# Layer 1 of a four-layer network: Silu of u and of the gate as x(1 + tanh(x/2))/2, the last product on VectorE, the halves in weights

## The chip, the core and the metric

The kernel runs on one core of one Trainium2 chip. The metric is the device time of one execution in microseconds, from start to end. Five engines work beside each other, each with its own queue in its own fixed order: PE (TensorE, matrix products), DVE (VectorE), ACT (ScalarE, which evaluates functions from tables), POOL (GpSimd) and SP (SyncE, which issues transfers). Matrix results lie in PSUM, everything else that engines work on lies in SBUF.

## The reference, cut to what matters

Four layers follow each other on an image tensor of 4 x 64 x 64 pixels with 192 channels, each as x + layer(groupnorm(x)). Layers 0 and 3 scan the image in four directions over its whole length, layer 2 multiplies with Toeplitz matrices. Layer 1, in which the change lies, runs one small state-space block over every row and every column, forwards and backwards, so in four directions:

```python
def mamba_block(xs, in_w, cw, cb, xw, dtw, dtb, Alog, Dv, ow):
    xz = jnp.einsum('nlc,dc->nld', xs, in_w)
    u, z = jnp.split(xz, 2, axis=-1)                 # 384 channels each
    ...                                              # 4 taps along the line
    uc = silu(uc + cb[None, :, None])
    x_dbl = jnp.einsum('nld,ed->nle', uc, xw)
    dt, Bp, Cp = jnp.split(x_dbl, [DT_RANK, DT_RANK + DS], axis=-1)
    delta = jax.nn.softplus(jnp.einsum('nlr,dr->nld', dt, dtw) + dtb)
    A = -jnp.exp(Alog)
    # per step: h = exp(delta * A) * h + (delta * u) * B ;  y = sum over 16 states of h * C
    y = jnp.moveaxis(ys, 0, 1) + uc * Dv
    y = y * silu(z)
    return jnp.einsum('nld,cd->nlc', y, ow)
```

silu(x) is x * sigmoid(x), which is x(1 + tanh(x/2))/2. The four results are concatenated and multiplied with one more weight, fc_w; the kernel multiplies fc_w into each out_w beforehand. All data are 32-bit floats.

## The kernel before, in words

Layer 1 is the method mamba. It first normalises x and stores it by rows and by columns, and builds the four combined output weights both_w (lines 737 to 747). Then it works through 128 chunks: four directions, four images, eight chunks of 512 pixels (eight lines of 64). A chunk is a job (mamba_job). Its 384 channels lie in three tiles t of 128.

A chunk has 24 units (t, p, c), one for each half tile of 64 channels and each of four groups of states. A unit is one scan over 128 x 1024 elements, and passes through the engines like this:
- feed (line 354): for 18 of the 24 units PE multiplies the matrices diag with dtuT into the PSUM tile b (line 378; two such buffers exist), and ACT computes dA = exp(delta * A) twice, 504 elements each (line 401), into one of three fixed SBUF tiles. For the other six ("direct") units POOL has multiplied delta * u with B into the SBUF tile bs (line 351), and ACT writes dA into the PSUM tile b.
- scan (line 411): DVE runs the recurrence into h, one of seven buffers; then POOL multiplies h with C in place (line 422).
- collect (line 447): PE sums over the states into y.

Around the units lie the steps of a chunk, each at a number of units counted from the chunk's first (the table when and the list steps, lines 896 to 901). Negative numbers lie in the time of the chunks before, so that several chunks are under way at once. The steps that matter here:
- input_of (steps -36, -34, -31): PE projects a tile of u into in_ps, and ACT scales it by the last tap (line 822). One step later DVE adds the three other taps from PSUM (line 827). Another step later ACT applies Silu with the bias conv_b (line 833).
- project (-24, line 209): PE multiplies u with x_w, which gives dt, B and C.
- finish (-14): ACT applies Softplus to delta (line 271), and POOL forms dtu = delta * u (line 278). In layers 0 and 3 the same line runs on DVE.
- gate (-6, -4, -1): PE projects a tile of the gate into z_ps. One step later ACT applies Silu (line 843).
- gated, after the last scan of a tile: DVE forms u * D + y (line 856, y in PSUM), POOL multiplies with z (line 857).
- out (33, 35): PE multiplies with the combined output weight into o_ps (line 881), and the result goes to memory through an SBUF tile of the name o.
- weights (-50 of a direction's first chunk) loads the direction's weights, and neg_exp turns A into -exp(A) (lines 453 and 454, ACT and DVE).

in_ps, z_ps, o_ps, the projections of step sizes and the transposes share two PSUM buffers (the pool mm). The pool pin has two buffers for each name, so two for o.

The order in which the work is written out follows the steps; a scheduler then fixes each engine's queue when the program is built. Where ACT needs a function whose table isn't loaded, an ACT_TABLE_LOAD stands in front of it in ACT's queue, under the line of the function.

Of the kernel before, what the change touches and what calls it, by code (L numbers as in the profile page):

```python
# [7 lines left out]
F32 = mybir.dt.float32  # L8
AF = mybir.ActivationFunctionType
ALU = mybir.AluOpType  # L10
# [9 lines left out]
T = 512  # L20
# [16 lines left out]
class Kernel:  # L37
# [670 lines left out]
    def mamba(self, x_in):  # L708

        tc, nc, ins = self.tc, self.nc, self.i  # L710
        P, NT = 128, 3
        DI = P * NT
        pre = "L1_"
        by_row, by_col = self.image_tiles("m_row"), self.image_tiles("m_col")
        done = [[self.dram.tile([C, L], F32, name=f"m_out{i}_{b}") for b in range(B)] for i in range(2)]

        both_w = [self.dram.tile([P, NT, C], F32, name=f"m_both_w{i}") for i in range(4)]
        bufs = dict(c=5, bc=2, diag=4, both=4, dtu2=3)
        with (
            tc.tile_pool(name="n", bufs=2) as pn,  # L720
            tc.tile_pool(name="n_ps", bufs=2, space=PSUM) as psum,
        ):
            for b in range(B):
                x = pn.tile([PC, KC, L], F32, name="x")
                for k in range(KC):
                    nc.sync.dma_start(x[:, k, :], x_in[b][:, k, :])
                self.group_norm(x, pn, psum)
                nc.sync.dma_start(by_row[b], x)
                xt = pn.tile([PC, KC, L], F32, name="xt")
                for k in range(KC):  # L730
                    nc.vector.tensor_copy(
                        xt[:, k, :].rearrange("p (a b) -> p a b", b=HW),
                        x[:, k, :].rearrange("p (a b) -> p b a", b=HW),
                    )
                nc.sync.dma_start(by_col[b], xt)
            fw = self.load(pn, "fw", ins["L1_fc_w"], bufs=1)
            for i, part in enumerate((4, 6, 0, 2)):
                ow = self.load(pn, "ow", ins["L1_out_w"][i])
                both = pn.tile([P, NT, C], F32, name="both_w")
                for t in range(NT):  # L740
                    ps = psum.tile([P, C], F32, name="both_ps")
                    for k in range(KC):
                        nc.tensor.matmul(
                            ps, ow[:, k, t * P : (t + 1) * P], fw[:, part + k, :], start=k == 0, stop=k == KC - 1
                        )
                    nc.scalar.copy(both[:, t, :], ps)
                nc.sync.dma_start(both_w[i], both)

        with (
            tc.tile_pool(name="m_once", bufs=1) as once,  # L750
            tc.tile_pool(name="m_w", bufs=2) as pw,
            tc.tile_pool(name="m_in", bufs=2) as pin,
            tc.tile_pool(name="m_prep", bufs=2) as prep,
            tc.tile_pool(name="m_work", bufs=2) as work,
            tc.tile_pool(name="m_c", bufs=bufs["c"]) as cp,
            tc.tile_pool(name="m_bc", bufs=bufs["bc"]) as bcp,
            tc.tile_pool(name="m_diag", bufs=bufs["diag"]) as dp,
            tc.tile_pool(name="m_both", bufs=bufs["both"]) as both,
            tc.tile_pool(name="m_dtu2", bufs=bufs["dtu2"]) as dtu2,
            tc.tile_pool(name="m_mm", bufs=2, space=PSUM) as mm,  # L760
            tc.tile_pool(name="m_b", bufs=2, space=PSUM) as bp,
            tc.tile_pool(name="m_y", bufs=2, space=PSUM) as yp,
        ):
            pools = {"prep": prep, "work": work, "c": cp, "diag": dp, "both": both, "mm": mm, "b": bp, "y": yp,
                     "bc": bcp, "dtu2": dtu2, "bufs": bufs, "behind": 3, "lag": 1}
            fixed = [once.tile([P, 2 * T], F32, name=f"dA{j}") for j in range(3)]
            zero = once.tile([P, 2 * ROWS], F32, name="zero")
            nc.gpsimd.memset(zero, 0.0)
            jobs = []
            for i in range(4):  # L770
                rev, w = i % 2 == 1, {}
                xs = by_row if i < 2 else by_col
                for b in range(B):
                    for c in range(NCH):
                        begin = b == 0 and c == 0
                        jobs.append(self.mamba_job(
                            pw, pin, mm, i, begin, rev, w, xs[b], done[i // 2][b], both_w[i], c, fixed, zero
                        ))
            self.run_jobs(jobs, pools)
        return list(zip(*done))  # L780

    def mamba_job(self, pw, pin, mm, i, begin, rev, w, x, done, both_w, c, fixed, zero):

        nc, ins = self.nc, self.i
        P, NT = 128, 3
# [3 lines left out]
        job = {}  # L789

        def weights():
            for name in ("in_w", "conv_w", "conv_b", "A", "D", "x_w", "dt_b"):
                w[name] = self.load(pw, name, ins[pre + name][i])
            w["dtw"] = self.load(pw, "dt_w", ins[pre + "dt_w"][i])
            w["out_w"] = self.load(pw, "out_w", both_w)
            w["xw"], w["dtb"] = w["x_w"], w["dt_b"]
            self.neg_exp(w["A"])

        def load():
            job["xn"] = self.load(pin, "xn", x[:, :, s])  # L800
            job["u"] = pin.tile([P, NT, T], F32, name="u", bufs=3)

        def project(t, to, name):
            ps = mm.tile([P, T], F32, name=f"{name}_ps", tag="mm")
            for k in range(KC):
                for half in range(2):
                    first = to + t * P + half * 64
                    nc.tensor.matmul(
                        ps[half * 64 : (half + 1) * 64, :], w["in_w"][:, k, first : first + 64], job["xn"][:, k, :],
                        start=k == 0, stop=k == KC - 1,  # L810
                    )
            return ps
# [3 lines left out]
        def input_of(t):  # L816
            ps = project(t, 0, "in").rearrange("p (a b) -> p a b", b=HW)
            u = job["u"][:, t, :].rearrange("p (a b) -> p a b", b=HW)
            tap = lambda j: w["conv_w"][:, t, j : j + 1]

            def taps():
                nc.scalar.activation(u, ps, AF.Identity, scale=tap(3))  # L822
                for j in range(1, 4):
                    to, of = slice(j, HW), slice(0, HW - j)
                    if rev:
                        to, of = of, to
                    nc.vector.scalar_tensor_tensor(  # L827
                        u[:, :, to], ps[:, :, of], tap(3 - j), u[:, :, to], ALU.mult, ALU.add
                    )
                return last  # L830

            def last():
                nc.scalar.activation(u, u, AF.Silu, bias=w["conv_b"][:, t : t + 1])

            return taps

        def gate(t):
            ps = project(t, DI, "z")

            def after():  # L840
                if t == 0:
                    job["z"] = pin.tile([P, NT, T], F32, name="z")
                nc.scalar.activation(job["z"][:, t, :], ps, AF.Silu)

            return after

# [49 lines left out]
        when = dict(project=-24, turn_b=-22, step_size=(-21, -19, -18), finish=-14, turn=(-9, -3, 8), store=-11)  # L896
        each = lambda f, ats: [(at, lambda t=t: f(t)) for t, at in enumerate(ats)]
        steps = [(-50, weights)] if begin else []
        steps += [(-46, load)] + each(input_of, (-36, -34, -31)) + each(gate, (-6, -4, -1)) + each(out, (33, 35))
        if rev:  # L900
            steps += each(earlier, (25, 28))
        job.update(
            P=P, NT=NT, DI=DI, w=w, rev=rev, carry=None, first=True, dA=fixed, y={}, fed={}, done={}, bs={},
# [326 lines left out]
```

## Time and profile before

| | |
|---|---|
| time, median of 3 runs | 30885.05 us (30880.78 to 30885.68) |
| the profiled execution, its own time | 30865.86 us |
| its span, first to last instruction | 30864.0 us |
| mean granted TensorE clock | 0.961 |
| layer 1's chunks, about | 10809 to 21708 us |
| busy in the span: PE, DVE, ACT, POOL | 87%, 72%, 75%, 74% |
| busy in layer 1's chunks (10899 us): PE, DVE, ACT, POOL | 9707, 7956, 9107, 9849 us |

Durations are those of the profiled execution. A line of the groups gives the source line, the engine, the operation, what it writes and reads with shapes, and the count; after the first bar the busy time and the mean duration of one in ns; after the second the time that the engine stood idle just before such instructions, and what ended it. A line of the timeline gives the start in us, the duration in us (of a run of like instructions together), engine, line, operation, tiles, count, and in brackets the idle time before it with its releaser. A line of a stretch gives its bounds and length, then the busy time of PE, PEld (the weight loads of PE), DVE, ACT and POOL with their instruction counts, the granted PE clock, the busy share of the DMA engines and GB/s.

### The profile page before, as it was taken

The numbers are of one execution on the slowest core, as the hardware profiler recorded it, in microseconds if no ns is written. First come the engines' busy times: TensorE is split into PE (matmuls) and PEld (weight loads), VectorE is DVE, ScalarE is ACT, GpSimd is POOL, SyncE is SP. The second block draws the span as 40 slices with busy tenths as digits, with TensorE's granted clock in tenths as the row PEclk, the third lists the DMA queues.
The fourth block names the chain that finished last, engine by engine and source line by source line (L and its number), as shares of the span: only waits on it lengthen the run. The fifth ranks groups of instructions, "written<-read, shape, count | busy, mean of one in ns | idle before, by whom it ended". The sixth has DMA issues, their size and how long they took to land. (4 is left out here: it accounts for less than half of the span.)

```text
span 30864.0 us, 503255 instructions
## 1 busy us (share of the span) xinstructions
PE 26878.4 (87%) x189464; PEld 15827.7 (51%) x189464; DVE 22327.6 (72%) x16587; ACT 23000.6 (75%) x50177; POOL 22890.6 (74%) x9831
## 2 busy tenths in 40 slices
PE   8998998999899688888888888888588988888888
PEld 5664665666466444444444444444355444444444
DVE  7887888788788777777777777777423267777777
ACT  7885886788588588888888888888232278788888
POOL 7885885888588499989998999999100077777777
PEclk9999999999999899999999999999788999999999
DMA  3334333433433533333333333333533345545454
GB/s 109 100 99 117 101 98 104 112 100 99 119 101 97 142 99 97 97 100 101 101 104 97 98 97 99 102 101 102 131 78 76 104 131 131 132 130 134 128 135 128
DMA packets 1652695, 3342.38 MB, mean 108 GB/s; under 512 B 396725, under 2 KB 453494, under 8 KB 1634646
## 3 DMA queue, kind: packets, MB, share of 16 engines
q1 hardware_dynamic: 1541718, 3142.34, 38.1%
q10 hardware_dynamic: 108544, 167.85, 1.6%
q8 instruction: 1497, 24.53, 0.4%
q14 instruction: 936, 7.67, 0.1%
HBM read 2149.81 MB, written 656.08 MB: 91 GB/s over the span
## 5 line engine op out<-in xcount | busy, mean ns | idle before, releaser
L378 PE MATMUL b<-diag,dtuT 128*64 128x256 f32 x98304 | 12607.9, 386 | 1732.9 <-DVE h L411 917.9
L422 POOL TENSOR_TENSOR hc<-h,c 128x1024 f32<-128x1024 f32 x4608 | 10943.4, 2395 | 1515.0 <-DVE h L418 1158.3
L378 PEld LDWEIGHTS b<-diag,dtuT 128*64 128x64 f32 x98304 | 8214.9, 138 | 6212.3 <-DVE h L411 1903.3
L401 ACT ACTIVATE dA<-both,A 128x512 f32<-128x512 f32 (+1 forms) x12288 | 8267.7, 711 | 2124.3 <-DVE h L411 1472.0
L418 DVE TENSOR_TENSOR_SCAN h<-dA,carry,b 128x512 f32<-128x512 f32 x6720 | 8169.8, 1263 | 1367.8 <-PE b L378 861.4
L422 POOL TENSOR_TENSOR h<-h,c 128x1024 f32<-128x1024 f32 x3072 | 7219.1, 2374 | 1049.2 <-DVE h L411 880.3
L332 ACT ACTIVATE diag<-ident,bt 128x128 f32<-128x128 f32 x20480 | 6570.6, 391 | 92.2 <-issue 91.4
L447 PE MATMUL y<-hc,fold 128*64 128x512 f32 x18432 | 5783.3, 599 | 386.1 <-POOL hc L422 384.4
L411 DVE TENSOR_TENSOR_SCAN h<-dA,b 128x1024 f32<-128x1024 f32 x2304 | 5202.8, 2274 | 1147.3 <-ACT dA L401 798.4
L351 POOL TENSOR_TENSOR bs<-dtu,bc 128x1024 f32<-128x1024 f32 x1536 | 3639.4, 2369 | 158.5 <-DMA c<-bc_dram 72.8
L447 PE MATMUL y<-h,fold 128*64 128x512 f32 x12288 | 3259.6, 593 | 10.2 <-POOL h L422 10.2
L501 POOL MEMSET pad<- 128x13068 f32 (+1 forms) x8 | 73.4, 9172 | 3968.3 <-DMA inw<-in_L_in_w 2997.7
L411 DVE TENSOR_TENSOR_SCAN h<-b,bs 128x1024 f32<-128x1024 f32 x768 | 1758.9, 2290 | 1413.6 <-ACT b L401 1102.8
L447 PEld LDWEIGHTS y<-hc,fold 128*64 128x64 f32 x18432 | 1924.0, 138 | 1550.1 <-POOL hc L422 813.1
L401 ACT ACTIVATE b<-both,A 128x504 f32<-128x504 f32 (+1 forms) x3072 | 2076.2, 676 | 376.4 <-DVE h L418 328.3
L418 DVE TENSOR_TENSOR_SCAN h<-b,carry,bs 128x512 f32<-128x512 f32 x1344 | 1639.2, 1260 | 220.9 <-issue 170.4
L237 PEld LDWEIGHTS dtu_ps<-ident,dtu 128*64 128x64 f32 (+1 forms) x16384 | 1183.2, 141 | 497.6 <-issue 375.9
L447 PEld LDWEIGHTS y<-h,fold 128*64 128x64 f32 x12288 | 1005.0, 137 | 795.2 <-issue 444.9
L418 DVE TENSOR_TENSOR_SCAN h<-dA,b 128x512 f32<-128x512 f32 x960 | 1112.8, 1205 | 352.8 <-PE b L378 191.3
L401 ACT ACT_TABLE_LOAD x1019 | 1307.4, 1283 | 11.8
L237 PE MATMUL dtu_ps<-ident,dtu 128*64 128x128 f32 (+1 forms) x16384 | 1272.7, 273 | 45.9 <-DVE dtu L278 41.5
L827 DVE SCALAR_TENSOR_TENSOR u<-in_ps,conv_w,u 128x504 f32<-128x504 f32 (+2 forms) x1152 | 831.6, 722 | 411.7 <-ACT u L822 402.6
(157 smaller groups left out, 24601.4 us busy)
## 6 DMA issues: line engine op xcount, KB each, us to landing
c<-bc_dram SPq DMA_DIRECT2D x3072, 256.0 KB, 4.1
both<-delta SPq DMA_DIRECT2D x2048, 128.0 KB, 2.7
bc<-bc_dram SPq DMA_DIRECT2D x768, 256.0 KB, 4.2
both<-delta_dram SPq DMA_DIRECT2D x1536, 128.0 KB, 3.7
dtu<-dtu_dram SPq DMA_DIRECT2D x1536, 128.0 KB, 2.7
dtu<-dtu SPq DMA_DIRECT2D x1280, 128.0 KB, 2.5
L_y<-out ACTq DMA_DIRECT2D x512, 256.0 KB, 3.0
u<-L_u SPq DMA_DIRECT2D x160, 768.0 KB, 5.4
```

The costliest lines, as they stand in the source:

```text
L237: nc.tensor.matmul(to[half * 64 : (half + 1) * 64], of[:, half * 64 : (half + 1) * 64], self.ident[:p, :p], start=True, stop=True,)
L332: nc.scalar.activation(to, self.ident, AF.Copy, scale=of)
L351: self.nc.gpsimd.tensor_mul(by(b), dtu, by(job["bbc"][p]))
L378: nc.tensor.matmul(to, dtu, job["diag"][p][:, k, 2 * q : 2 * q + 2, :], start=True, stop=True,)
L401: nc.scalar.activation(to[n], of, AF.Exp, scale=w["A"][:, g, 2 * p + n : 2 * p + n + 1])
L411: nc.vector.tensor_tensor_scan(h[:, way], dA[:, way], b[:, way], 0.0, ALU.mult, ALU.add)
L418: nc.vector.tensor_tensor_scan(hn[:, n, way], dA[:, n, way], by_n[:, n, way], start, ALU.mult, ALU.add)
L422: nc.gpsimd.tensor_mul(hc, h, job["cbc"][p])
L447: nc.tensor.matmul(y[c * 64 : (c + 1) * 64, :], self.fold, of, start=first == 0 and n == 0, stop=last == LAST and n == 1)
L501: nc.gpsimd.memset(pad, 0.0)
L827: nc.vector.scalar_tensor_tensor(u[:, :, to], ps[:, :, of], tap(3 - j), u[:, :, to], ALU.mult, ALU.add)
```

## The change

Silu is no longer taken from ACT's table. For u, ACT adds the bias in the first Identity (line 822 before), later computes tanh(u/2) into an SBUF tile of the ring o, and one step later DVE forms (tanh + 1) * u, both from SBUF. For the gate, ACT computes tanh(z/2) from z_ps into z, and one step later DVE forms (tanh + 1) * z_ps, the second input from PSUM. Both results are twice the Silu. The half of u is put into x_w, which DVE halves once for each direction; the remaining uses of u and the gate carry factors of two that the output weight takes back: the 12 evacuations of both_ps multiply by 0.25. (delta * u, like B and C, enters the sum together with x_w's results, so that y is twice what it was, as is u * D.)

```diff
@@ mamba: both_w
-                    nc.scalar.copy(both[:, t, :], ps)
+                    nc.scalar.mul(both[:, t, :], ps, 0.25)
@@ mamba_job: weights
             w["xw"], w["dtb"] = w["x_w"], w["dt_b"]
             self.neg_exp(w["A"])
+            nc.vector.tensor_scalar_mul(w["xw"], w["xw"], 0.5)
@@ mamba_job: input_of
             def taps():
-                nc.scalar.activation(u, ps, AF.Identity, scale=tap(3))
+                nc.scalar.activation(u, ps, AF.Identity, bias=w["conv_b"][:, t : t + 1], scale=tap(3))
...
             def last():
-                nc.scalar.activation(u, u, AF.Silu, bias=w["conv_b"][:, t : t + 1])
+                u = job["u"][:, t, :]
+                half = pin.tile([P, T], F32, name="o")
+                nc.scalar.activation(half, u, AF.Tanh, scale=0.5)
+
+                def doubled():
+                    nc.vector.scalar_tensor_tensor(u, half, 1.0, u, ALU.add, ALU.mult)
+
+                return doubled
@@ mamba_job: gate
-                nc.scalar.activation(job["z"][:, t, :], ps, AF.Silu)
+                z = job["z"][:, t, :]
+                nc.scalar.activation(z, ps, AF.Tanh, scale=0.5)
+
+                def doubled():
+                    nc.vector.scalar_tensor_tensor(z, z, 1.0, ps, ALU.add, ALU.mult)
+
+                return doubled
```

A function that a step returns is called one step later, ahead of that step's own work.

## The prediction

> **What bounds the kernel now.** I read the page first (which engines are busy), then the groups of instructions over the stage that the change touches, then busy time by stretch, then the timeline of one chunk. The stage of layer 1 runs from about 10809 to 21708 us: 128 chunks. GpSimd's product of delta and u comes once a chunk, first at 10789.7 and last at 21597.3 us, so a chunk takes 10807.6 / 127 = 85.1 us. Groups of the stage (line, engine, operation, count | busy, mean ns | idle before, releaser):
>
> ```profile
> L422 POOL TENSOR_TENSOR h<-h,c 128x1024 f32<-128x1024 f32 x3069 | 7212.1, 2374 | 1049.2 <-DVE h L411 880.3 <-PE in_ps L808 155.1 <-PE y L447 12.6
> L401 ACT ACT_TABLE_LOAD x761 | 976.4, 1283 | 8.7
> L843 ACT ACT_TABLE_LOAD x382 | 490.1, 1283 | 6.8
> L833 ACT ACT_TABLE_LOAD x252 | 323.3, 1283 | 4.0 <-DVE u L827 1.1
> L271 ACT ACT_TABLE_LOAD x127 | 162.9, 1283 | 2.3
> ```
>
> Twelve table loads a chunk: six back to Exp, three for the gate's Silu, two for u's, one for Softplus. Next, busy time in one chunk, then in the two stretches of it (stretch, length, PE, PEld, DVE, ACT, POOL):
>
> ```profile
> 14999.38:15084.72 85.34, 76.08 (x550) 39.31 (x552) 62.61 (x39) 71.08 (x133) 77.05 (x34) 1.00 0.35 102
> 15001.70:15051.80 50.10, 44.56 (x330) 24.07 (x328) 37.70 (x24) 37.50 (x70) 50.10 (x23) 1.00 0.36 111
> 15051.80:15084.70 32.90, 29.18 (x200) 13.52 (x197) 22.57 (x15) 32.48 (x63) 24.64 (x12) 1.00 0.35 93
> ```
>
> In the first stretch POOL is never idle. In the second ACT is never idle (32.5 of 32.9 us) and POOL loses 8.3 us. The timeline shows the chain there: ACT is late, the scan waits for it, POOL waits for the scan.
>
> ```profile
> 15066.46 1.28 ACT L843 ACT_TABLE_LOAD   x1
> 15067.76 0.60 ACT L843 ACTIVATE z<-z_ps 128x512 f32<-128x512 f32 x1
> 15070.69 1.28 ACT L401 ACT_TABLE_LOAD   x1
> 15073.33 2.29 DVE L411 TENSOR_TENSOR_SCAN h<-dA,b 128x1024 f32<-128x1024 f32 x1 [4.57 <-ACT dA L401]
> 15082.30 2.29 DVE L411 TENSOR_TENSOR_SCAN h<-b,bs 128x1024 f32<-128x1024 f32 x1 [3.82 <-ACT b L401]
> 15075.70 2.36 POOL L422 TENSOR_TENSOR h<-h,c 128x1024 f32<-128x1024 f32 x1 [2.59 <-DVE h L411]
> 15084.72 2.37 POOL L422 TENSOR_TENSOR h<-h,c 128x1024 f32<-128x1024 f32 x1 [3.80 <-DVE h L411]
> ```
>
> **What the Trainium skill says.** "ScalarE: Activation LUTs", Table sets: Exp and Tanh lie in one set, and a switch of set costs a load of 1283 ns plus a drain of some 1380 ns. The trace agrees on 1283 and shows no such drain: one load, Silu, load takes 3.33 us (15043.90 to 15047.23), 1.30 per load. I use 1.30. "SBUF — State Buffer", Who interferes with whom: a VectorE instruction with two SBUF inputs, or in a two-port mode, excludes a GpSimd instruction that reads SBUF. The trace agrees, with a difference between the two kinds that decides one rival:
>
> ```profile
> 26774.37 2.34 POOL L422 TENSOR_TENSOR hc<-h,c 128x1024 f32<-128x1024 f32 x1
> 26774.79 3.00 DVE L278 TENSOR_TENSOR dtu<-delta,u 96x1024 f32<-96x1024 f32 x1 [0.50 <-ACT delta L271]
> 26776.68 3.34 POOL L422 TENSOR_TENSOR hc<-h,c 128x1024 f32<-128x1024 f32 x1
> 13575.84 8.25 DVE L454 TENSOR_SCALAR A<-A 128x48 f32<-128x48 f32 x1
> ```
>
> The two-input product (1.19 us when undisturbed, the shortest of its line) waited out one POOL instruction, then ran ahead of the next one, which was stretched from 2.37 to 3.34. The tensor_scalar, 0.19 us alone, was passed by four POOL instructions and got in when POOL ran dry.
>
> **The change, part by part.**
> 1. *Loads.* In the instruction order of the changed kernel L401 keeps 383 loads of 1019, L271 its 384, and the two Silu lines' 637 shrink to one. So 10 of 12 loads a chunk go: 10 x 1.30 = 13.0 us of ACT, eight of them (10.4 us) in the second stretch. ACT there falls to about 22 us and stops being what ends last.
> 2. *The functions.* Tanh of the gate is taken at Silu's 597 ns. Tanh of u loses its bias pointer and Identity gains one. No trace row has either form; the difference of Silu with bias from SBUF (722) and without from PSUM (597) bounds it at about 0.12 us each, of opposite sign: 0 net, 0.4 us a chunk at most, covered by ACT's slack.
> 3. *Gate's product on VectorE*, three a chunk. One input is in PSUM, as in L856 (723 ns, some 0.64 start to start): 1.9 us. In one of the two shared PSUM buffers, z_ps is now held until VectorE is done, behind a scan (2.28 us) on its queue; what waits is the next projection on PE, and behind it the b matmuls. Today PE waits 1.2 us a chunk for the gate's Silu. Bounds: -1.2 (the loads ahead of it are gone) to +5.6 (two waits of a scan and a product). I take +0.5.
> 4. *u's product on VectorE*, three a chunk, two SBUF inputs. 0.7 own (L856 has its size), and by L278's example 0 to 2.4 of waiting for the running POOL instruction, 1.1 in the mean: 5.4 us of VectorE a chunk. POOL is held about 0.5 each time, 1.5 a chunk. Below: 0, if POOL is idle at that moment. VectorE comes to 62.6 + 1.9 + 5.4 = 70 us a chunk.
> 5. *x_w halved*, a tensor_scalar from SBUF to SBUF, once per direction; two of four fall into the running stage, as L454's two do. L454 stalled VectorE 8.25 and 7.96 us, after which POOL idled 2.3 + 3.3 us. I take 5.6 each, 11 us in all (0 to 20).
> 6. *Nothing:* the 0.25 goes into the 12 copies of both_ps; the tanh's buffer is the o ring (2 buffers), whose other uses lie at other steps of the chunk, covered by steps of over 3 us between them; the PSUM output of the taps is read no later than before. If the o ring were taken, the wait would be that of a 2 to 3 us store, once or twice a chunk.
>
> No DMA is added or moved past another in the steady part.
>
> **The sum.** POOL's own work sets a floor: 77.05 + 1.5 = 78.5 us a chunk. The second stretch alone can't fall to POOL's 24.6 us, since PE has 29.2 us of work in it and VectorE 22.6 + 1.9 + 3.6 = 28. With only two b buffers these two wait for each other: 29.2 + 0.5 + some 1.3 of mutual waits = 31. If nothing carries over between stretches, a chunk is 2.3 (the instruction ahead of the first stretch) + 50.1 + 0.5 + 31 = 83.9. But POOL enters the second stretch 4.4 us behind VectorE (its queue ends at 15051.84, the scan before at 15047.4), and this lead can grow once ACT isn't late. So a chunk lies between 78.5 and 83.9; I take the middle, 81.2. Gain: (85.1 - 81.2) x 128 = 499 us, less 11 for part 5, is 488. The profiled execution took 30865.9 us (span 30864.0); that gives 30378. The median of the runs, 30885, is 19 above it: 30397.
>
> **Rivals.**
> - *POOL's floor is reached* (22 in 100). For: 50 us without idle in the first stretch, although Softplus's two loads lie in it. Against: PE's 29.2 us. 78.5 us a chunk: 845 - 11 = 834 gained, 30051.
> - *The second stretch stays slow, with VectorE and PE in the place of ACT* (20 in 100). For: 28 and 29.2 us on in-order queues that feed each other. Against: POOL's lead. 83.9 us: 154 - 11 gained, 30742.
> - *Starvation, slower* (8 in 100). u's product is served like L454: only when POOL has run dry. Each then costs POOL 0.64 + 2.28 + 0.1 = 3.0 us (product, next scan, semaphore), three a chunk: 77.05 + 9.1 = 86.1, so +130 us and part 5, 31026; if PE's excess in the second stretch isn't covered by the same idle, up to 90 us a chunk, 31500. It decides from 2.7 us of POOL idle each, (85.1 - 77.05) / 3. For: L454. Against: L278 above, served after one instruction, and L545 beside POOL's copies likewise.
> - *The change doesn't do what it says*, if Tanh lay in another set than Exp: the order above, with its loads gone, excludes it.
>
> **How the numbers follow.** The likeliest case, 80 to 82.4 us a chunk, has 45 in 100 and its own range 30240 to 30550; the floor has 22, the slow stretch 20, starvation 8, and 5 lie about no change (gains of layer 1 lost to a new wait that I don't see). The range 30020 to 30760 leaves out starvation, no change, and the ends of the floor and slow cases. About 0.2%, 62 us, is what a measurement tells from no change; the cases faster by more are 0.45 + 0.22 + 0.20 = 0.87, same 0.05, slower 0.08.
>
> **What would show it.** Right: some 1270 loads fewer; ACT near 58 us a chunk; POOL over 93% busy in the stage; u's product at 0.7 to 3.1 us, with POOL instructions stretched after it; the scan's waits on ACT in the second stretch gone, its waits on PE's b grown. Wrong: products of u of 5 us and more (starvation); PE idle behind the gate's product (part 3 mis-sized); POOL still 90% busy with VectorE busy beside it (the slow stretch).

## The result, and the profile after

The changed kernel takes 30864.08 us in the median (30852.44 to 30871.02, 12 runs), the kernel before beside it 30880.62 (30867.93 to 30888.63, 12 runs). The ratio is 0.9994, with an interval of 0.9986 to 1.0002: no change that a measurement can tell, where a gain of 488 us was forecast. The profiled execution has a span of 30858.5 us, and POOL's product of delta and u comes at 10790.6 the first time and at 21591.1 us the last, so a chunk takes 10800.5 / 127 = 85.04 us, after 85.10.

Yet the loads that the change was to remove are gone. First the groups of the stage, 10809 to 21708 us, as for the kernel before (busy us, mean ns | idle before, releaser):

```profile
L422 POOL TENSOR_TENSOR h<-h,c 128x1024 f32<-128x1024 f32 x3072 | 7325.7, 2402 | 948.3 <-DVE h L411 915.8 <-issue 29.3 <-DMA dtu<-dtu_dram 2.3
L839 DVE SCALAR_TENSOR_TENSOR u<-o,u 128x512 f32<-128x512 f32 x378 | 807.4, 2136 | 0.0
L855 DVE SCALAR_TENSOR_TENSOR z<-z,z_ps 128x512 f32<-128x512 f32 x382 | 257.8, 675 | 238.7 <-ACT z L852 238.7
L271 ACT ACT_TABLE_LOAD x127 | 162.9, 1283 | 2.3
L401 ACT ACT_TABLE_LOAD x127 | 162.9, 1283 | 2.3
```

Two table loads a chunk are left of twelve. L422 still stands idle 916 us for VectorE's scans, where it was 880. And the two new products differ by a factor of three though they do the same arithmetic on the same sizes: 675 ns with one input in PSUM (L855), 2136 ns with both in SBUF (L839).

Busy time in one chunk (length, PE, PEld, DVE, ACT, POOL, PE's clock); the same view before is the chunk from 14999.38 in the prediction:

```profile
15021.16:15106.42 85.26, 76.28 (x550) 38.74 (x548) 70.28 (x45) 58.27 (x123) 77.88 (x36) 0.96 0.35 101
```

ACT has fallen from 71.1 to 58.3 us and VectorE has risen from 62.6 to 70.3, both as the sum said. POOL has 77.9 of 85.3 us, after 77.1. The waits in 12000 to 20000 us (engine and line, what it waited for, total us, times, longest) say what took ACT's place. Three of them before, then those after:

```profile
DVE h L411 <- ACT b L401: 821.8, 302, 4.7
POOL h L422 <- DVE h L411: 654.8, 285, 4.1
DVE h L411 <- ACT dA L401: 574.5, 272, 4.6
```

```profile
PE b L378 <- DVE h L411: 839.5, 340, 6.9
POOL h L422 <- DVE h L411: 667.6, 374, 4.2
DVE h L411 <- ACT b L401: 431.3, 187, 4.4
DVE h L411 <- PE b L378: 299.6, 422, 2.3
DVE h L411 <- ACT dA L401: 54.0, 44, 1.6
```

The scan's waits for ACT were 574.5 (dA) and 821.8 us (b) before, so two thirds of them went. POOL's wait for the scan was 654.8 and is 667.6 us: nothing of what VectorE no longer waits for has reached POOL. The timeline of one chunk shows where it stays (start, duration, engine, line; in brackets the idle time before and its releaser):

```profile
15039.75 7.00 POOL L422 TENSOR_TENSOR h<-h,c 128x1024 f32<-128x1024 f32 x3
15040.41 2.28 DVE L411 TENSOR_TENSOR_SCAN h<-dA,b 128x1024 f32<-128x1024 f32 x1
15042.60 4.71 DVE L839 SCALAR_TENSOR_TENSOR u<-o,u 128x512 f32<-128x512 f32 x1
15047.23 1.50 DVE L828 SCALAR_TENSOR_TENSOR u<-in_ps,conv_w,u 128x504 f32<-128x504 f32 x2
15048.65 2.28 DVE L411 TENSOR_TENSOR_SCAN h<-dA,b 128x1024 f32<-128x1024 f32 x1
15051.00 2.37 POOL L422 TENSOR_TENSOR h<-h,c 128x1024 f32<-128x1024 f32 x1 [4.25 <-DVE h L411]
15050.98 3.68 PE L378 MATMUL b<-diag,dtuT 128*64 128x256 f32 x16 [6.51 <-DVE h L411]
```

POOL has three products in a row, the last ending at 15046.76. VectorE comes to the product of u's first tile at 15042.60, while the second of them runs. It isn't served at 15044.46 when that one ends; the third goes ahead of it, and it ends at 15047.31, when POOL has run dry. Two taps and a scan stand behind it. So POOL idles 4.25 us and PE 6.51 us, until the scan of 15048.65 has read the PSUM tile b. This happens once in each chunk: of the 384 products of u 124 are passed by one POOL instruction in this way and take 4.7 to 5.1 us, one is passed by two (6.9 us), and all but two of the other two tiles' take 0.67 to 0.9.

### The profile page after: what moved, and what is told of

It is laid out like the page before. It is cut to its first block, busy times and chain, and to the rows that moved or that the text cites. A ratio compares the mean times of both kernels' runs of the same rounds, so it can differ in the third digit from the quotient of the medians.

```text
span 30858.5 us, 502565 instructions
## 1 busy us (share of the span) xinstructions
PE 26908.0 (87%) x189464; PEld 15624.6 (51%) x189464; DVE 23308.9 (76%) x17359; ACT 21412.5 (69%) x48905; POOL 23003.0 (75%) x9831
## 4 chain that ended last, share of the span: by engine, by line
PE 35%; DVE 23%; ACT 21%; POOL 8%; issue 6%; DMA 5%; SPq 1%; ACTq 0%; DVEq 0%; POOLq 0%
PE b L378 16%; DVE h L411 9%; ACT dA L401 7%; ACT diag L332 7%; PE y L447 6%; DVE h L418 6%; POOL h L422 4%; DVE u L828 2%; DVE u L839 2%; POOL bs L351 2%; ACT b L401 2%; PE yt_ps L1094 2%; PE conv_ps L533 2%; DMA xn<-t_xn 2%; PE o_ps L1064 1%
## 5 line engine op out<-in xcount | busy, mean ns | idle before, releaser
L422 POOL TENSOR_TENSOR hc<-h,c 128x1024 f32<-128x1024 f32 x4608 | 10947.2, 2396 | 1504.1 <-DVE h L418 1175.8
L422 POOL TENSOR_TENSOR h<-h,c 128x1024 f32<-128x1024 f32 x3072 | 7325.7, 2402 | 948.3 <-DVE h L411 915.8
L447 PEld LDWEIGHTS y<-h,fold 128*64 128x64 f32 x12288 | 898.7, 141 | 670.4 <-issue 332.6
L278 DVE TENSOR_TENSOR dtu<-delta,u 128x1536 f32<-128x1536 f32 (+1 forms) x256 | 563.6, 2202 | 604.9 <-ACT delta L271 604.7
```

The lines of the kernel that those rows point to most:

```text
L422: nc.gpsimd.tensor_mul(hc, h, job["cbc"][p])
L447: nc.tensor.matmul(y[c * 64 : (c + 1) * 64, :], self.fold, of, start=first == 0 and n == 0, stop=last == LAST and n == 1)
```

## The experiments

Had the loads been worth little, or had they been worth what was forecast and something else eaten it? Theory P says the second, and puts the loss into that product of u with two SBUF inputs. Its rivals put it into the added work of VectorE and ScalarE, or into the queue order, which the scheduler fixes anew when instructions change. The recorded expectations call the rivals of a run D and C and say there what each means; Q, R, S and N are named where they come up. "Us a chunk" is the distance of the first and last L278 on POOL, divided by 127; every ratio is against the kernel before on the same chip.

| kernel | median us | ratio, interval | us a chunk |
|---|---|---|---|
| before | 30855 to 30868 | 1 | 85.10 |
| loads_gone | 30256.1 | 0.9804 (0.9789 to 0.9818) | 80.33 |
| psum_half | 30449.6 | 0.9871 (0.9856 to 0.9886) | 81.86 |
| before_plus_add | 31523.7 | 1.0220 (1.0203 to 1.0237) | 90.33 |
| u_only | 30721.6 | 0.9959 (0.9944 to 0.9973) | 84.02 |
| gate_only | 30124.2 | 0.9765 (0.9751 to 0.9780) | 79.25 |
| u_psum_only | 30448.6 | 0.9866 (0.9849 to 0.9882) | 81.81 |
| psum_ring4 | 30446.0 | 0.9864 (0.9849 to 0.9878) | 81.81 |
| gate_ring4 | 30014.3 | 0.9725 (0.9710 to 0.9739) | 78.43 |
| psum_split | 30451.2 | 0.9866 (0.9849 to 0.9882) | 81.87 |
| psum_early | 30463.6 | 0.9870 (0.9855 to 0.9884) | 81.87 |
| gate_split | 30141.3 | 0.9764 (0.9750 to 0.9779) | 79.54 |
| psum_dve_tap | 30035.9 | 0.9732 (0.9715 to 0.9748) | 78.52 |

### The product with one input in PSUM: psum_half

The changed kernel, with tanh(u/2) written into the PSUM buffer in_ps, which is free by then, and not into an SBUF tile. (ACT can do that: in the direct units it writes dA into PSUM too.) The order of VectorE's queue is that of the changed kernel in all but 7 of 17359 places, POOL's in all but 2 of 9831, ACT's in all but 64 of 48905; PE's was not compared. In the cut below flat is the whole of in_ps.

```diff
-                half = pin.tile([P, T], F32, name="o")
+                half = flat
                 nc.scalar.activation(half, u, AF.Tanh, scale=0.5)
```

> Edit to the changed kernel: tanh(u/2) is written into in_ps (PSUM), which is dead after the third tap, so u's product on VectorE has one SBUF input; its place in VectorE's order is the same. Theory P (the two-input product is starved once a chunk, 4.7 us at the first tile of u, and that gives the table loads' gain back): the first product falls from 4.7-5.1 to 0.7 us, POOL's idle of 4.2 us behind it goes, a chunk falls from 85.0 to 80-82 us, the time to 30350-30500. Rival D (VectorE and PE, with their mutual waits, would have kept the stretch slow anyway): the product falls too, but waits on PE's b or on ACT's u take its place, a chunk stays at 84-85, time 30750-30880. Rival C (the PE clock, 0.96 in the stage after against 1.00 before, eats it): PE's busy time a chunk grows and the clock stays at 0.96 or less, no gain.

Measured: 30449.6 us. The line of u's product (min/median/max ns) in this kernel, then in the changed kernel:

```profile
L840 DVE SCALAR_TENSOR_TENSOR u<-in_ps,u x384: 658/665/691, 10767.7 to 21143.3; 128x512 f32<-128x512 f32 x192
```
```profile
L839 DVE SCALAR_TENSOR_TENSOR u<-o,u x384: 665/854/6949, 10773.6 to 21550.8; 128x512 f32<-128x512 f32 x192
```

All 384 now take the same 0.67 us, and 85.04 - 81.86 = 3.2 us a chunk come back, where D had forecast a chunk of 84 to 85 us and C no gain. That confirms P: beside the place of the second input, what differs is those few places of the queues, and that in_ps is held until the product is done. The latter has a price of its own (PE waits 232 us in all for these products, 1.8 us a chunk), so the 3.2 us are what is left after it. It agrees with the Trainium skill, "SBUF — State Buffer", Who interferes with whom: a VectorE instruction with at most one SBUF input, outside the two-port modes, doesn't contend with GpSimd.

### The same cost put on the kernel before: before_plus_add

The kernel before, with a VectorE instruction of two SBUF inputs after u's Silu, which adds zeros to u (none is a view of a tile of zeros).

```diff
             def last():
                 nc.scalar.activation(u, u, AF.Silu, bias=w["conv_b"][:, t : t + 1])
+
+                def again():
...
+                    nc.vector.scalar_tensor_tensor(flat, none, 1.0, flat, ALU.mult, ALU.add)
+
+                return again
```

> Edit to the kernel before: all Silus stay, and one step after u's Silu VectorE adds a zero tile to u (two SBUF inputs, 512 elements), three a chunk; the values don't change. The suspected cost by itself. Theory P: one of three is starved for about 4 us a chunk, POOL idles behind it; a chunk grows by 2-4 us, time 31150-31400. Rival D: three times 0.7 us, hidden beside ACT: within 0.3% of before.

Measured: 31523.7 us, 5.2 us a chunk more than before, above what was expected. Its additions wait more often:

```profile
L841 DVE SCALAR_TENSOR_TENSOR u<-zeros,u x384: 659/2656/9149, 10769.9 to 22213.5; 128x512 f32<-128x512 f32 x192
```

The median is 2656 ns and not 854, and the longest waits 9.1 us. So the price of one such instruction isn't fixed. Compared with POOL's queue in the traces, some 250 of these 384 wait out the POOL instruction that is running and go ahead of the next one, 123 let one more pass (4.1 to 4.4 us) and one lets three pass. In the changed kernel 127 wait out the running one, 125 are passed and 132 find POOL idle. What decides is not settled. All of those passed once or twice stand between two L422 on POOL; nearly all of those that were not passed (in the changed kernel 126 of 127) stand between two different lines. But in the trace before, all 243 L278 of VectorE that met a running L422 with another one behind it were served after the first.

### The loads alone: loads_gone

The kernel before with Tanh in Silu's place, in the same two lines. The products and the halves are left out; nothing is added.

```diff
-                nc.scalar.activation(u, u, AF.Silu, bias=w["conv_b"][:, t : t + 1])
+                nc.scalar.activation(u, u, AF.Tanh, bias=w["conv_b"][:, t : t + 1])
...
-                nc.scalar.activation(job["z"][:, t, :], ps, AF.Silu)
+                nc.scalar.activation(job["z"][:, t, :], ps, AF.Tanh)
```

> Edit to the kernel before: Silu is replaced by Tanh on ACT at both places and nothing is added; the products with 1 + tanh and the halves are left out, so u and the gate are tanh alone. What the ten loads a chunk are worth without any price. Theory P (the loads' worth is there, and was paid back by products and their places in the queues): GpSimd nearly saturated, a chunk at 77.5-79.5 us, 29950-30200. Rival D (the second stretch stays bound by PE and VectorE whatever ACT does): 83-84 us, 30650-30800.

Measured: 30256.1 us, 4.8 us a chunk less than before, and 56 us above the upper end of what was expected. On the way from before over loads_gone and psum_half to the changed kernel the steps are, in us a chunk: the loads 80.33 - 85.10 = -4.8; both products, without the conflict, and the rest of the change 81.86 - 80.33 = +1.5; the conflict 85.04 - 81.86 = +3.2. That they add up to -0.1 follows from how they are taken and shows nothing by itself; on another way the shares can differ, as the next runs show.

### One half of the change at a time: gate_only, u_only, u_psum_only

gate_only is the kernel before with the gate alone as tanh and product. u_only is the changed kernel with the gate's Silu put back, and u_psum_only is psum_half with the gate's Silu put back. In all three both_ps is multiplied by 0.5. The cut is from u_only and u_psum_only; gate_only makes the same change of lines the other way round, on the kernel before.

```diff
-                z = job["z"][:, t, :]
-                nc.scalar.activation(z, ps, AF.Tanh, scale=0.5)
...
-                    nc.vector.scalar_tensor_tensor(z, z, 1.0, ps, ALU.add, ALU.mult)
...
+                nc.scalar.activation(job["z"][:, t, :], ps, AF.Silu)
```

> Edit to the kernel before: only the gate is taken by tanh, with its product on VectorE (one input in PSUM); u keeps Silu. Four of the twelve loads a chunk go (380 at u's Silu, 762 at Exp are left in the order). Theory P: 5 us of ACT in the second stretch gone, no two-SBUF product: POOL's idle falls by 3-5 us a chunk, time 30300-30550. Rival D: VectorE's three more products and the longer hold of z_ps take it up, time 30800-30900.

> Edit to the changed kernel: the gate has its Silu again, u alone is taken by tanh with the two-SBUF product on VectorE. Loads: 384 at the gate's Silu and 767 at Exp, eight of twelve a chunk stay. Theory P: the starved product (4-5 us once a chunk) stands against 5 us of loads, and the gate's loads still hold ACT in the second stretch: 31000-31400, slower than before. Rival D: the two-SBUF product costs only its own 0.7 us: 30550-30750.

> Edit to the changed kernel: the gate has its Silu again; u is taken by tanh, written into in_ps, so its product has one SBUF input. Against u_only (30722) this takes the two-input wait away. Theory P: by the 3.2 us a chunk that psum_half gained over the changed kernel, 30250-30400. Rival D (with the gate's loads on ACT the wait was covered): 30600-30730.

Measured: gate_only 30124.2 us, better than expected and better than loads_gone, although it keeps eight loads a chunk of twelve. u_only comes to 30721.6, faster than before, where P had said slower. The time lies in D's range, but D's reason doesn't hold: the product doesn't cost its own 0.7 us alone, since it starves once a chunk (4.5 to 5.1 us, 123 times) as in the changed kernel. Its four loads fewer pay more than that. Against u_only, u_psum_only is faster by 273 us (2.2 us a chunk), between the two expectations: the conflict's cost is confirmed but smaller than in the full change.

Two things can't be explained by loads and conflict. psum_half and u_psum_only take the same time, so once u is changed the gate's six loads, less the gate's product, are worth nothing. And gate_only, with four loads fewer than before, is 2.6 us a chunk faster than psum_half with ten fewer. There is a second limit, and it comes with u.

### The second limit: the rings, and the order of the taps

The waits that differ are VectorE's for the first tap of u, ACT's Identity (12000 to 20000 us; psum_half, then gate_only, then before):

```profile
DVE u L829 <- ACT u L824: 557.2, 293, 2.4
```
```profile
DVE u L827 <- ACT u L822: 303.6, 202, 2.0
```
```profile
DVE u L827 <- ACT u L822: 281.2, 187, 2.0
```

Three times a chunk in psum_half, u_psum_only (5.7 us a chunk each) and loads_gone (6.0), twice in gate_only and before (3.0), and twice in the changed kernel too, where one tile's taps stand behind the held-up product and find the Identity done (15047.23 in its timeline). A chunk of loads_gone shows how such a wait comes about:

```profile
15046.69 2.27 DVE L411 TENSOR_TENSOR_SCAN h<-dA,b 128x1024 f32<-128x1024 f32 x1
15049.00 1.32 ACT L401 ACTIVATE dA<-both,A 128x504 f32<-128x504 f32 x2 [0.87 <-DVE h L411]
15050.32 0.68 ACT L822 ACTIVATE u<-in_ps,conv_w 128x512 f32<-128x512 f32 x1
15051.03 1.51 DVE L827 SCALAR_TENSOR_TENSOR u<-in_ps,conv_w,u 128x504 f32<-128x504 f32 x2 [2.07 <-ACT u L822]
```

The taps stand behind the scan of 15046.69 on VectorE. The Identity stands on ACT behind a pair of dA that waits for the dA tile which that same scan frees. So VectorE, just done with the scan, waits out 1.32 + 0.68 us of ACT: 2.07 us here, 2.0 in the mean of this kernel.

Theory Q: ACT can't run ahead because only three dA tiles exist. psum_ring4 and gate_ring4 have four, paid for with one buffer of C fewer. R is the rival that VectorE and PE are too dense, so that the waits only move to PE's b. (The "Rival S" of these two expectations is the price of the lost C buffer; it is not the theory S below.)

```diff
-        bufs = dict(c=5, bc=2, diag=4, both=4, dtu2=3)
+        bufs = dict(c=4, bc=2, diag=4, both=4, dtu2=3)
...
-            fixed = [once.tile([P, 2 * T], F32, name=f"dA{j}") for j in range(3)]
+            fixed = [once.tile([P, 2 * T], F32, name=f"dA{j}") for j in range(4)]
```

> Edit to psum_half: four fixed dA tiles in place of three, one C buffer fewer (4 for 5) to make room; VectorE's order around u is the same. Theory Q (what still separates psum_half, 30450, from gate_only, 30124, is that u's taps stand on VectorE right behind a scan and wait for the Identity on ACT, which stands behind a dA pair that waits for that scan to give a dA tile back): the taps' wait on the Identity, 2.1 us each and three a chunk, falls below 1 us, time 30050-30250. Rival R (VectorE's six products and PE's work in the second stretch are too dense): the waits move to PE's b, time 30400-30500. Rival S: the lost C buffer makes POOL wait for transfers, slower than psum_half.

> Edit to gate_only: four dA tiles for three, four C buffers for five. GpSimd idles only 2 us a chunk in gate_only (30124), so theory P: at most 1-2 us a chunk more, 29880-30100. Rival S: the lost C buffer costs, 30124-30400.

Measured: psum_ring4 30446.0 us, no change, with 293 waits for the Identity (501 us in the stretch, after 557): Q falls for this kernel. The scan's waits for PE's b grew from 237 to 585 us, as R had said. gate_ring4 gains 110 us over gate_only, as was expected, and reaches 78.43 us a chunk. It does so with more waits for the Identity than gate_only, three a chunk and 3.9 us:

```profile
DVE u L827 <- ACT u L822: 394.1, 306, 2.0
```

So the number of these waits alone doesn't say how fast a kernel is.

Theory S: it is the taps' place in VectorE's queue. Three kernels write the taps one step later (psum_split, gate_split) or the Identity one step earlier (psum_early); psum_split also writes u's product in the step of its tanh. N is the rival that the waits are slack: without them another wait takes their place.

```diff
             def taps():
                 nc.scalar.activation(u, ps, AF.Identity, bias=..., scale=tap(3))
+                return others
+            def others():
                 for j in range(1, 4):
                     ...
```

> psum_half with the three taps on VectorE put one step later than ScalarE's Identity of the same tile (same instructions, another order). In psum_half VectorE waits for that Identity 293 times in 8000 us, 2.4 us each, 5.7 us a chunk of 81.9, against 3.0 us a chunk of 79.3 in gate_only. Theory S (the place of the taps in VectorE's queue is what keeps psum_half 2.6 us a chunk behind gate_only): these waits fall under 1 us a chunk, the chunk comes to 79.0 to 80.3 us, 30080 to 30250 us. Rival N (VectorE's waits there are slack that another wait takes over, on PE's b or on ScalarE's dA): the waits for the Identity go and the time stays at 30390 to 30510.

> psum_half with ScalarE's Identity of u put one step earlier, right behind PE's projection, the taps where they were. Theory S: as in psum_split the taps find the Identity done, 30080 to 30250 us. Rival N: 30390 to 30510. If psum_split gains and this doesn't, it is ScalarE that is held up by the Identity (its wait for PE's projection) and the order on ScalarE that matters.

> gate_only with the three taps on VectorE one step later than the Identity. gate_only's POOL idles only 2.1 us a chunk, so the gain has that bound. Theory S: the Identity waits (2.0 us, 202 times in 8000 us) go, 29850 to 30050 us. Rival N: 30070 to 30180.

Measured: 30451.2, 30463.6 and 30141.3 us, no gain in any. But the waits didn't go either: 294 for the Identity in both psum kernels (559.3 and 559.7 us). VectorE's queue in psum_split and psum_early is the same as in psum_half, and gate_split's the same as gate_only's, instruction for instruction; in psum_early and gate_split those of POOL and ACT are too. The scheduler put the taps in the same places, whatever step they were written in. So these three decide nothing between S and N. The two whose queues are the same lie 14 and 17 us from the kernels that they come from, which shows what a difference of that size is worth.

So the last kernel takes away what makes the taps wait. psum_dve_tap is psum_half with the first tap on VectorE too; apart from that added instruction VectorE's order differs from psum_half's in 15 of 17359 places.

```diff
-                nc.scalar.activation(u, ps, AF.Identity, bias=w["conv_b"][:, t : t + 1], scale=tap(3))
+                nc.vector.tensor_scalar(u, ps, tap(3), w["conv_b"][:, t : t + 1], ALU.mult, ALU.add)
```

> psum_half with the first tap of u (ScalarE's Identity with scale and bias, 0.76 us) computed on VectorE instead, as a tensor_scalar from PSUM, so that the other taps, next on VectorE's queue, wait for no other engine. VectorE gains some 0.7 us of work three times a chunk, 2.1, and loses the waits for the Identity, 5.6 us a chunk. Theory S (these waits are what holds psum_half 2.6 us a chunk behind gate_only): 79 to 80.6 us a chunk, 30080 to 30300 us. Rival N (the waits are slack; what is missing is taken by waits for PE's b and for h, and VectorE's added work comes on top): 81.5 to 83.5 us a chunk, 30390 to 30670 us.

Measured: 30035.9 us, 414 less than psum_half, more than S had said. Busy time in 12000 to 20000 us (length, PE, PEld, DVE, ACT, POOL, clock), psum_half and then psum_dve_tap:

```profile
12000.00:20000.00 8000.00, 7319.01 (x53360) 3715.56 (x53358) 6404.39 (x4195) 5693.00 (x11997) 7516.76 (x3321) 0.99 0.35 104
```
```profile
12000.00:20000.00 8000.00, 7539.44 (x55670) 3874.17 (x55666) 6894.32 (x4676) 5722.49 (x12178) 7833.23 (x3463) 1.00 0.36 108
```

VectorE does 490 us more in the stretch, and the kernel is faster; POOL is busy 98% of the time. A chunk takes 78.52 us. 0.79 us more work on VectorE, three times a chunk, bought the end of 5.7 us of waits, and POOL's waits for the scan fell from 457.6 us in the stretch to

```profile
POOL h L422 <- DVE h L411: 130.3, 172, 1.0
```

So S forecast the right side and N falls: the waits were not slack. That they alone held psum_half back is not shown, since the edit also takes the Identity's 2.3 us a chunk out of ACT's queue. (ACT is idle for 29% of this stretch in psum_half, but where it stands in its order can still matter.) And gate_ring4 is as fast with such waits in it: there POOL waits 68 us for the scan, so it has enough finished scans ahead of it to bridge them. That last step is argued, not tried.

psum_dve_tap, with the whole change in it, and gate_ring4, with the gate's half, are the fastest, 2.7% below the kernel before, at 78.5 and 78.4 us a chunk. The floor of 78.5 that the prediction gave POOL is the same number by chance: 1.5 us of it were for the conflict, which neither has. POOL's own work is 76.9 and 76.8 us a chunk in them.

## Why the prediction was wrong, point by point

**The bound, and part 1, the loads: right.** Ten of twelve loads a chunk went, ACT came to 58.3 us (58 forecast), and by themselves they were worth 4.8 us a chunk. 71.1 - 58.3 us over ten loads is 1.28 each, so no drain shows here either. (In the Trainium skill, "ScalarE: Activation LUTs", the drain's figure stands in the section What ACT_TABLE_LOAD costs and not under Table sets.)

**Part 2, the functions: right.** Tanh of u takes 624 ns (Silu 722), the Identity with bias 768 (667 without), tanh of the gate 577 (597): together within 0.1 us.

**Part 3, the gate's product: right in size.** 675 ns. The hold of z_ps, put at +0.5 us a chunk, shows no cost: PE and its weight loads waited 0.3 us in the whole run for this product. VectorE waits 239 us in the stage for ACT's tanh ahead of it, 1.9 us a chunk, which was not in the sum. What these are worth in time was not tried apart; they lie in the 1.5 us a chunk between loads_gone and psum_half.

**Part 4, u's product: the step that failed.** It was put at 0.7 us and 0 to 2.4 us of waiting, 1.1 in the mean, by L278, which waited out one POOL instruction. The mean was not far off: 2136 ns measured against 1.8 us. What was wrong is the upper end and the assumption that it is spread. The waits come as one of 4 us a chunk, because the product can be passed by POOL's next instruction and is then served when POOL has run dry. Then VectorE is late at the very moment when POOL has no scan left to work on, and the delay goes through to POOL (4.25 us idle) and PE (6.51). It costs 3.2 us a chunk where 1.5 of POOL's time had been put down. The page "SBUF — State Buffer", Who interferes with whom, says of the two-port modes that whoever issues first has the shared ports for the whole instruction while the other blocks; here the blocked one also lost its turn to an instruction that was queued later. The rival "starvation" named this mechanism from L454, at 8 in 100, with three cases a chunk; it was one in three. L278 and L454 both stood in the trace, and the sum took the kinder. For L278 it had 243 cases, all served after one POOL instruction; what failed is that they were taken to hold for another instruction at another place.

**Part 5, x_w: over-sized.** In the running stage L798, the halving, takes 1.8 and 0.6 us of VectorE, where 5.6 us of lost time each had been put down. L454, which had stalled 8.25 and 7.96 us before, takes 0.2 and 0.7 here, which the sum did not have either.

**The sum.** Without the conflict the forecast would have stood: psum_half, which is the change without it, measures 30449.6 us and 81.9 us a chunk, inside the likeliest case's range (80 to 82.4). That is luck: 81.2 was the middle of two bounds (part 3's 0.5 entered the upper one twice; with it once the middle is 80.95), and the reason given isn't the one that the runs show. The second stretch was said to be held by PE and VectorE feeding each other through two b buffers; the runs show a wait of VectorE for ACT's Identity, which is more frequent without the loads (twice a chunk before, three times in loads_gone and psum_half). psum_dve_tap, without it, has POOL busy for 98% of the stretch, with the same two b buffers and more work on VectorE.

**One term was missing.** PE's clock (the column after POOL's) in the chunk above:

```profile
15044.00:15047.00 3.00, 0.47 (x4) 0.00 (x0) 3.00 (x1) 2.97 (x9) 2.76 (x2) 1.00 0.00 0
15047.00:15050.00 3.00, 0.00 (x0) 0.00 (x0) 2.96 (x4) 1.68 (x6) 0.00 (x0) 0.74 0.00 0
15052.00:15053.00 1.00, 1.00 (x8) 0.60 (x6) 1.00 (x1) 1.00 (x3) 1.00 (x1) 0.50 0.06 16
15056.00:15058.00 2.00, 2.00 (x14) 0.81 (x12) 0.99 (x1) 0.97 (x2) 2.00 (x2) 1.00 0.34 86
```

PE fell idle at 15044.47. From about 15048.4 it has half its clock, and the full one again from 15055.3. The sixteen matmuls of b in between take 3.68 us, where they take 1.95 at full clock. So this stall of PE lengthened itself by 1.7 us. The mean clock of 12000 to 20000 us shows it: 1.00 before, 0.95 after, 0.99 in psum_half. How much of the 3.2 us is owed to the clock was not tried apart.

## What to carry to other kernels

A VectorE instruction with two SBUF inputs, beside a GpSimd that never rests, should be costed by its worst wait at its place in the queue, not by a mean; put one input into PSUM, here a buffer that was free anyway. When loads or other work go from an in-order engine, look for the producer that stands there behind something which waits for the consumer's own last instruction. Here moving the step in the source left VectorE's queue as it was, and giving that work to the consumer itself gained 414 us. Test the halves of a change apart, since here their gains did not add up.

## What the runs showed of the hardware that was not expected

- A VectorE instruction of 0.66 us with both inputs in SBUF took up to 9.1 us beside a busy GpSimd (before_plus_add). In the changed kernel 125 of 384 were passed by an instruction that GpSimd had queued behind the one then running, while in the trace before none of 243 L278 was. In psum_half, with one of the inputs in PSUM, none of 384 took over 0.69.
- PE's clock halves a few us after PE has fallen idle and comes back a few us after it starts again: 4.0 and 4.3 us in the chunk above, 4.1 and 4.4 one chunk later (half clock from 15133.8 to 15140.6, PE idle 6.53 us up to 15136.26). Over the 93 such stalls in 12000 to 20000 us of the changed kernel the clock fell after 2.1 to 5.4 us (median 3.9) and came back after 3.5 to 5.8 (median 4.8). The Trainium skill states this under "TensorE: Matmul & The Clock Gate", What's actually happening: half rate after an idle window of about 3.4 us, the full rate after about as long at work. The two medians lie 0.5 and 1.4 us above that. The spells of half clock came in steps: 6.83 us (62 of 96 in that stretch), 10.24 (31) and 3.41 (3). Shorter stalls can start one too: psum_half has 98 stalls of 3.3 us in the same stretch and 49 spells, 36 of them of 3.4 us.
- Work moved from ScalarE to VectorE, the busier of the two, made the kernel faster: VectorE rose from 80% to 86% busy in psum_dve_tap, and the kernel became 414 us shorter.
